# FFN weight preparation in a decoder layer: 16 conversions to bfloat16 moved to GpSimd, 14 PSUM copies moved to ScalarE

## The chip, the cores and the metric

The kernel runs on one core of a Trainium2 chip. The metric is the device time of one execution in microseconds (us). A core has a matrix engine (TensorE, in the profile PE, with its weight loads listed apart as PEld), three engines for elementwise work (VectorE or DVE, ScalarE or ACT, GpSimd or POOL) and a sync engine (SP) that here only issues DMAs. Each engine takes its instructions strictly in the order of the program and waits for the others by semaphores. TensorE writes only to PSUM, which has eight banks; VectorE and ScalarE can read PSUM.

## The reference: what is computed

One decoder layer on x of shape (4, 1024, 256), in float32. Three blocks follow each other, each on a layer norm of x and added to x:

```python
x = x + attn(layernorm(x), w_qkv, w_out)            # 16 heads of 16, windows of 128 plus the window before
x = x + xattn(layernorm(x), ctx, ctx, mask, Wq, ...)  # 77 context rows
x = x + ffn(layernorm(x), clip_x, clip_down, w_gate, w_up, w_down)

def weight_fake_quant(w):                            # in the FFN, per row of w
    scale = max(abs(w), axis=1) / 127
    return clip(round(w / scale), -128, 127) * scale

xq = act_fake_quant(x, clip_x)                       # one scale for the whole tensor
h = act_fake_quant(silu(xq @ wq(w_gate).T) * (xq @ wq(w_up).T), clip_down)
return h @ wq(w_down).T
```

w_gate and w_up are (704, 256), w_down is (256, 704). The quantised weights are whole numbers from -128 to 127, which bfloat16 holds exactly; the row scales are multiplied in later.

## The kernel before

**Two phases.** Up to about 600 us the kernel does self attention (S) and cross attention (X) for four batches; the rest is the FFN. The attention is cut into eight jobs, in the order S0, S1, S2, X0, S3, X1, X2, X3. A job has four groups of four heads, written (g, o), and a group is cut into units: four for S, two for X. There are 96 units, and one slot of the schedule handles one unit, some 4 to 7 us.

**A slot** is written out by hand, in this order of program text, and so of each engine's queue: early layer norms `xn` on GpSimd (L529); then `weighted_values` into a bank `ps_av` for a group whose weights are two slots old, with its copy, normalising and transposes on VectorE (L780 to L802); then `tasks`; then `beside` (work off TensorE); then `put_maxima`, which transposes the row maxima into `ps_mx`, copies them on ScalarE to `mxT` (L683) and writes them by four DMAs on SP into spare rows of `q` (L686); then `max_bias` and `maxima` for the unit five slots ahead: scores into four banks `sc_n`, whose maxima VectorE takes (L657 for S, L668 for X); then `weight_bias` and `weights` for the unit of the slot: scores transposed into four banks `sc_t` (L712 for S; L697 and L741 for X), exp on ScalarE (L722, L744), and for S a causal select on GpSimd (L726). The `bo` additions on GpSimd (L556) come last. The maxima written by `put_maxima` are needed by `weights` in the next slot for an S group, three slots later for X.

**Tasks** have an earliest slot, a due slot and a cost, and the planner fits them in by due time up to a cap of 1.35 a slot on the first list and 1.2 on `beside`. Tasks on TensorE are the projections of q and k (`ps_p`, L583, out of PSUM by two ScalarE operations each, L593 to L599), the values (`ps_v`, L564, by ScalarE, L571), transposes of the normalised input (`ps_t`, L544, one half by VectorE, L548, the other by ScalarE, L550), the output projection (`ps_op`, L811, added to x by VectorE, L820), and the turns described next.

**The FFN weights** are prepared beside the attention by `prep_ffn`, in 14 pieces, one every three slots or so from job S2 on: six row blocks of 128 for w_gate, six for w_up (`rows_of`), two for w_down (`down`). Each piece has four steps. `load` fetches the rows by SP. `scale` (cost 1.0, in `beside`) takes their largest magnitude and its reciprocal on VectorE (L426 to L429). `quant` (cost 1.0, in `beside`) multiplies on VectorE to int8 (L435, into `w8`, which has one buffer) and converts to bfloat16 (L436, into `q_f` or `q_d`, two buffers); for w_down the last 64 columns are copied once more (L482), and the scale is spread to `wide` (L484). `turn` (cost 0.2, a task, due six to seven slots after the load) transposes on TensorE into one bank, `ps_f` for two blocks of 128 (L462) or `ps_d` for six (L489), and copies the bank into `wgT`, `wuT` or `wdT` (L465, L492), which the FFN reads after 600 us. For w_down `wide` is transposed too, into `ps_ds`, and copied by VectorE (L495).

**Banks.** All tiles named `ps_...`, `sc_n` and `sc_t` share the eight banks of one pool. The pool gives a new tile the bank that it reckons to be free first, and the first matmul into it waits for the last reader of the tile before. In the program before, the banks next used after the turns are these: in the slots at 276, 371 and 414 us `ps_f`'s bank goes to the second `sc_t` tile of the same slot and `ps_mx`'s to the fourth; at 291, 315, 429, 447 and 468 us `ps_f`'s or `ps_d`'s goes to the third; at 334 and 346 us to an `sc_n` tile of the next slot.

Of the kernel before, what the change touches and what calls it, by code (L numbers as in the profile page):

```python
# [17 lines left out]
P = 128  # L18
# [6 lines left out]
def decoder_layer(  # L25
# [32 lines left out]
    nc = tc.nc  # L58
    B, S, D = x.shape
    SK = ctx_in.shape[1]  # L60
    FF = w_gate.shape[0]
# [11 lines left out]
    HR = FF - (NF - 1) * P  # L73
# [73 lines left out]
    wdT = fw.tile([P, NF, D], BF16, name="wdT")  # L147
# [51 lines left out]
    with ExitStack() as att:  # L199
# [6 lines left out]
        def bank(name):  # L206
            return ps_b.tile([P, 512], F32, name=name, tag="b")
# [6 lines left out]
        for o in range(NS):  # L214
# [15 lines left out]
            q = wp.tile([P, 1], F32, name=f"qrows{o}")  # L230
# [8 lines left out]
        f = stage.tile([P, P], F32, name="cb_f", tag="stage")  # L239
# [183 lines left out]
        def row_scale(raw, rows, scale_out):  # L423

            a = small.tile([P, 1], F32, name="wamax")
            nc.vector.tensor_reduce(a[:rows], raw, AX.X, ALU.max, apply_absolute_value=True)  # L426
            nc.vector.tensor_scalar(scale_out, a[:rows], 1.0 / QMAX, None, ALU.mult)
            inv = small.tile([P, 1], F32, name="winv")
            nc.vector.reciprocal(inv[:rows], scale_out)  # L429
            return inv  # L430

        def quantise_rows(raw, rows, inv, q):

            q8 = small.tile([P, FF], I8, name="w8", bufs=1)[:rows, : raw.shape[1]]
            nc.vector.tensor_scalar(q8, raw, inv[:rows], None, ALU.mult)  # L435
            nc.vector.tensor_copy(q, q8)  # L436

        def prep_ffn():


            def rows_of(w, dst, sc, f):
                kept = {}

                def load():
                    kept["raw"] = stage.tile([P, D], F32, name="raw_f", tag="stage")
                    if f < NF - 1:
                        nc.sync.dma_start(out=kept["raw"], in_=w[f * P : (f + 1) * P, :])
                    else:
                        for r in (0, HR):
                            nc.sync.dma_start(out=kept["raw"][r : r + HR], in_=w[f * P :, :])  # L450

                def scale():
                    kept["i"] = row_scale(kept["raw"], P, sc[:, f : f + 1])

                def quant():
                    kept["q"] = stage.tile([P, D], BF16, name="q_f", tag="stage_q")
                    quantise_rows(kept["raw"], P, kept["i"], kept["q"])

                def turn():
                    ps = ps_b.tile([P, NC, P], BF16, name="ps_f", tag="b")  # L460
                    for c in range(NC):
                        nc.tensor.transpose(  # L462
                            ps[:, c, :], kept["q"][:, c * P : (c + 1) * P], ident_bf
                        )
                    nc.vector.tensor_copy(dst[:, :, f * P : (f + 1) * P], ps)  # L465

                return [load, scale, quant, turn]

            def down(c):
                kept = {}  # L470

                def load():
                    kept["raw"] = stage.tile([P, FF], F32, name="raw_d", tag="stage")
                    nc.sync.dma_start(out=kept["raw"], in_=w_down[c * P : (c + 1) * P, :])

                def scale():
                    kept["i"] = row_scale(kept["raw"], P, dsc[:, c : c + 1])

                def quant():
                    kept["q"] = stage.tile([P, NF * P], BF16, name="q_d", tag="stage_q")  # L480
                    quantise_rows(kept["raw"], P, kept["i"], kept["q"][:, :FF])
                    nc.vector.tensor_copy(kept["q"][:, FF:], kept["q"][:, FF - HR : FF])  # L482
                    kept["w"] = stage.tile([P, P], F32, name="wide", tag="stage")
                    nc.vector.tensor_copy(kept["w"], dsc[:, c : c + 1].to_broadcast([P, P]))  # L484

                def turn():
                    ps = ps_b.tile([P, NF, P], BF16, name="ps_d", tag="b")
                    for f in range(NF):
                        nc.tensor.transpose(  # L489
                            ps[:, f, :], kept["q"][:, f * P : (f + 1) * P], ident_bf  # L490
                        )
                    nc.vector.tensor_copy(wdT[:, :, c * P : (c + 1) * P], ps)  # L492
                    ps = bank("ps_ds")
                    nc.tensor.transpose(ps[:, :P], kept["w"], ident)
                    nc.vector.tensor_copy(dsc_row[:, c * P : (c + 1) * P], ps[:, :P])  # L495

                return [load, scale, quant, turn]

            pieces = []
            for w, dst, sc in ((w_gate, wgT, gsc), (w_up, wuT, usc)):  # L500
                for f in range(NF):
                    pieces.append(rows_of(w, dst, sc, f))
            return pieces + [down(c) for c in range(NC)]
# [677 lines left out]
        ps = bank("ps_idle")  # L1181
# [289 lines left out]
```

## Time and profile before

| What | us |
|---|---|
| median of three runs (704.75 to 706.25) | 705.66 |
| the profiled execution, its own time | 707.16 |
| its span, first to last instruction | 705.5 |
| TensorE busy | 660.4 |
| VectorE busy | 548.9 |
| ScalarE busy | 364.8 |
| GpSimd busy | 267.3 |

The profile page gives busy time, the span in slices, the chain of waits that ended last, and groups of instructions. A group's line reads: source line, engine, operation, result <- operands, shapes, count, then busy us, mean ns of one, idle us of the engine just before, and what ended most of that idle time. In the chain view a piece is start, length, engine, tile, line. In the timeline a piece is start, length, engine, line, operation, and in brackets the idle time ahead of it with what ended it. A view of waits lists who waited for whom: total us, times, longest. The granted TensorE clock was 0.987 of full speed on average.

### The profile page before, as it was taken

What the parts mean: (1) busy time and instruction counts of PE and PEld (TensorE: products, weight loads), DVE (VectorE), ACT (ScalarE), POOL (GpSimd) and SP (SyncE); (2) the same over time, 40 slices, a digit from 0 to 9 for tenths busy, and PEclk for the clock granted to TensorE, in tenths of its full rate; (3) what the DMA queues carried; (4) which work ended last, traced back from release to release, by engine and by line L of the source; (5) the groups of instructions that cost most, each with busy time, mean ns of one, the idle gap of its engine ahead of it and who ended that gap; (6) DMA issues with size and microseconds to landing.
All of it is one profiled execution on the core that took longest, in us unless ns stands there. A gap on an engine that the chain in (4) does not pass through costs nothing.

```text
span 705.5 us, 17377 instructions
## 1 busy us (share of the span) xinstructions
PE 660.4 (94%) x6470; PEld 402.6 (57%) x6470; DVE 548.9 (78%) x1919; ACT 364.8 (52%) x670; POOL 267.3 (38%) x514
## 2 busy tenths in 40 slices
PE   7989999999999989999999999999999999778787
PEld 4557566667665666654567667544554537334553
DVE  5588778669788798667879977866766868789887
ACT  2544564634556436534464465345445474688391
POOL 4046533627236386700064788234411023111022
PEclk9999999999999999999999999999999999999999
DMA  8000100000000000000000000000000000000047
GB/s 291 8 3 11 35 3 17 3 20 19 12 15 9 10 10 11 20 2 17 3 9 25 26 24 24 3 2 4 17 17 3 18 17 16 0 2 0 1 90 150
DMA packets 18645, 17.02 MB, mean 24 GB/s; under 512 B 3788, under 2 KB 18049, under 8 KB 18561
## 3 DMA queue, kind: packets, MB, share of 16 engines
q1 hardware_dynamic: 16369, 14.08, 6.4%
q0 software_dynamic: 1904, 1.84, 2.1%
q8 instruction: 51, 0.84, 0.5%
q14 instruction: 33, 0.27, 0.1%
q10 hardware_dynamic: 288, 0.00, 0.0%
HBM read 9.35 MB, written 6.03 MB: 22 GB/s over the span
## 4 chain that ended last, share of the span: by engine, by line
PE 73%; DVE 15%; ACT 6%; issue 4%; DMA 1%; POOL 1%; SPq 0%; ACTq 0%; DVEq 0%
PE ps_p L583 12%; PE sc_n L627 8%; PE ps_av L756 8%; PE sc_t L712 8%; PE ps_op L811 7%; PE sc_n L642 4%; PE ps_av L766 4%; PE sc_t L741 3%; PE po L1397 3%; PE ps_v L564 3%; PE sc_t L697 3%; DVE junk L657 2%; PE ps_t L544 2%; DVE bnst L189 2%; PE pg L1288 2%
## 5 line engine op out<-in xcount | busy, mean ns | idle before, releaser
L657 DVE CUSTOM_DVE_ANT_0 junk<-sc_n,cboth 128x256 bf16<-128x256 f32 (+1 forms) x512 | 172.7, 403 | 39.6 <-PE sc_n L627 39.1
L722 ACT ACTIVATE pt<-sc_t 128x512 f32<-128x512 f32 (+1 forms) x256 | 125.3, 577 | 99.4 <-PE sc_t L712 96.8
L726 POOL TENSOR_SCALAR_AFFINE_SELECT pt<-pt 128x256 f32<-128x256 f32 x256 | 102.2, 408 | 117.1 <-ACT pt L722 106.8
L744 ACT ACTIVATE ptx<-sc_t 77x512 f32<-77x512 f32 x128 | 65.4, 591 | 77.4 <-PE sc_t L741 77.4
L712 PE MATMUL sc_t<-q,k 32*128 32x256 f32 (+1 forms) x1024 | 88.1, 381 | 2.3 <-DMA q<-mxT 0.9
L627 PE MATMUL sc_n<-k,q 32*128 32x256 f32 (+1 forms) x1024 | 80.4, 393 | 0.7 <-DVE mx L657 0.7
L668 DVE TENSOR_REDUCE mx<-sc_n 128x4 f32<-128x308 f32 x128 | 52.2, 470 | 37.0 <-PE sc_n L642 36.8
L157 POOL TENSOR_SCALAR ve<-mv 128x4 f32<-128x4 f32 x20 | 4.6, 232 | 197.7 <-DVE mv L191 197.6
L712 PEld LDWEIGHTS sc_t<-q,k 32*128 32x128 f32 x1024 | 67.1, 189 | 13.1 <-ACT q L597 2.3
L529 POOL TENSOR_SCALAR xn<-x,mv,rs 128x256 f32<-128x256 f32 x56 | 70.4, 1262 | 0.0
L627 PEld LDWEIGHTS sc_n<-k,q 32*128 32x128 f32 x1024 | 49.8, 186 | 30.3 <-DVE mx L657 11.0
L583 PE MATMUL ps_p<-xnT,w_s 128*128 128x512 f32 x128 | 62.4, 617 | 2.3 <-DVE mx L657 1.2
L780 DVE STREAM_TRANSPOSE o_sb<-ps_av 128x512 f32<-128x512 f32 x63 | 45.0, 714 | 23.2 <-PE ps_av L756 13.8
L756 PE MATMUL ps_av<-pt,vt 128*32 128x256 f32 (+1 forms) x1152 | 58.8, 347 | 2.4 <-DVE mx L657 2.3
L756 PEld LDWEIGHTS ps_av<-pt,vt 128*32 128x32 f32 x1152 | 34.6, 110 | 30.4 <-DVE mx L657 6.0
L657 DVE DVE_READ_ACCUMULATOR2_ANT mx<- 128x1 f32 x512 | 42.6, 83 | 0.0
L642 PEld LDWEIGHTS sc_n<-kx,q 32*128 32x128 f32 x1024 | 31.5, 186 | 14.5 <-issue 14.5
L697 PE MATMUL sc_t<-mb_t,ident_bf 77*77 77x512 bf16 x128 | 35.3, 379 | 4.0 <-ACT q L593 3.6
L583 PEld LDWEIGHTS ps_p<-xnT,w_s 128*128 128x128 f32 x128 | 22.5, 192 | 28.1 <-issue 17.1
L642 PE MATMUL sc_n<-kx,q 32*128 32x77 f32 x1024 | 36.2, 277 | 0.0
L766 PE MATMUL ps_av<-ptx,vx 77*32 77x512 f32 x256 | 35.2, 604 | 0.6 <-DVE mx L668 0.6
L1304 DVE SCALAR_TENSOR_TENSOR hT<-pu,usc,act 128x512 f32<-128x512 f32 x44 | 30.6, 744 | 6.4 <-ACT act L1303 6.4
(200 smaller groups left out, 1092.2 us busy)
## 6 DMA issues: line engine op xcount, KB each, us to landing
x<-in_x_dram SPq DMA_DIRECT2D x8, 512.0 KB
out_dram<-y SPq DMA_DIRECT2D x9, 256.0 KB
q<-mxT SPq DMA_DIRECT2D x128, 4.0 KB
out_dram<-x SPq DMA_DIRECT2D x7, 256.0 KB
out_dram<-y POOLq DMA_DIRECT2D x7, 256.0 KB, 4.5
w_s<-in_L_attn_w_qkv_dram SPq DMA_DIRECT2D x2, 384.0 KB
raw_d<-in_L_ffn_w_down_dram SPq DMA_DIRECT2D x2, 352.0 KB
raw_f<-in_L_ffn_w_gate_dram SPq DMA_DIRECT2D x5, 128.0 KB
```

The source lines that it names most:

```text
L529: eng.tensor_scalar(xn, xb[job.b][:, t, :], job.st[hf].mv[:, i, 0:1], job.st[hf].rs[:, i : i + 1], ALU.subtract, ALU.mult,)
L583: nc.tensor.matmul(ps, w[:, c, g * P : (g + 1) * P], job.xnT[hf][:, c, :], start=(c == 0), stop=(c == NC - 1),)
L627: nc.tensor.matmul(banks[j][:, (i + 1) * 2 * P - n : (i + 1) * 2 * P], q[r, t * P : (t + 1) * P], k[r, k0 * P : k0 * P + n], start=True, s ...
L642: nc.tensor.matmul(banks[j][:, i * SK : (i + 1) * SK], q[r, t * P : (t + 1) * P], k[r, :], start=False, stop=(i == HT - 1),)
L657: nc.vector.tensor_tensor_reduce(out=junk[:, 2 * P - n :], in0=banks[j][:, (i + 1) * 2 * P - n : (i + 1) * 2 * P], in1=cboth[:, 2 * P - n ...
L697: nc.tensor.matmul(banks[j][:SK], ident_bf[:SK, :SK], mb_t[:, s], start=True, stop=False)
L712: nc.tensor.matmul(banks[j][:, w : w + n], k[r, t * P : (t + 1) * P], q[r, t * P : t * P + n], start=True, stop=True,)
L722: nc.scalar.activation(pt.rearrange("p i a q -> p (i a q)")[:, :w], banks[j][:, :w], AF.Exp)
L726: nc.gpsimd.affine_select(out=pt[:, :, 0, :], in_=pt[:, :, 0, :], compare_op=ALU.is_ge, fill=0.0, base=0, pattern=[[0, 2], [1, P]], channe ...
L744: nc.scalar.activation(pt, banks[j][:SK], AF.Exp)
L756: nc.tensor.matmul(ps[j * SL : (j + 1) * SL, (a0 - t0) * P : (a1 - t0) * P], slot_of(job.vs[kb // 2][:, kb % 2], heads[j]), job.pts[g, o, ...
L766: nc.tensor.matmul(ps[j * SL : (j + 1) * SL, :], slot_of(vx[:, job.b], heads[j]), job.pts[g, o, j, hf], start=True, stop=True,)
```

## The change

Four statements inside the attention change their engine; their operands, order in the text and tiles stay.

```diff
@@ quantise_rows
             nc.vector.tensor_scalar(q8, raw, inv[:rows], None, ALU.mult)
-            nc.vector.tensor_copy(q, q8)
+            nc.gpsimd.tensor_copy(q, q8)
@@ rows_of, turn
-                    nc.vector.tensor_copy(dst[:, :, f * P : (f + 1) * P], ps)
+                    nc.scalar.copy(dst[:, :, f * P : (f + 1) * P], ps)
@@ down, quant
-                    nc.vector.tensor_copy(kept["q"][:, FF:], kept["q"][:, FF - HR : FF])
+                    nc.gpsimd.tensor_copy(kept["q"][:, FF:], kept["q"][:, FF - HR : FF])
@@ down, turn
-                    nc.vector.tensor_copy(wdT[:, :, c * P : (c + 1) * P], ps)
+                    nc.scalar.copy(wdT[:, :, c * P : (c + 1) * P], ps)
```

The first runs 14 times (12 of 256 columns, 2 of 704), the second 12 times (256 columns), the third twice (64 columns), the fourth twice (768 columns). The conversions then wait for VectorE's L435 in GpSimd's queue, the copies for TensorE's transposes in ScalarE's queue. Nothing else differs in the text.

## The prediction

> **What bounds the kernel now.** I read the page first: busy time, then the chain of waits.
>
> ```profile
> PE 660.4 (94%) x6470; PEld 402.6 (57%) x6470; DVE 548.9 (78%) x1919; ACT 364.8 (52%) x670; POOL 267.3 (38%) x514
> ...
> PE 73%; DVE 15%; ACT 6%; issue 4%; DMA 1%; POOL 1%; SPq 0%; ACTq 0%; DVEq 0%
> ```
>
> TensorE is the bound; VectorE holds 15% of the chain that ended last. Next, the groups by line: everything the change touches runs between 222 and 468 us. In the stretch 215 to 475 us the stretch view gives PE 251.84 busy us of 260, DVE 205.77, ACT 129.40, POOL 128.56. PE idles 8 us there, so no relief of another engine can be worth more than that. The chain drawn over the same stretch has 33.0 us of DVE, 2.9 of ACT and none of POOL.
>
> **What the change removes.** The groups that leave VectorE:
>
> ```profile
> L436 DVE CAST q_f<-w 128x256 bf16<-128x256 int8 x12 | 3.8, 320 | 0.4
> ...
> L465 DVE COPY wuT<-ps_f 128x256 bf16<-128x256 bf16 x6 | 1.7, 285 | 2.7 <-PE ps_f L462 2.7
> L465 DVE COPY wgT<-ps_f 128x256 bf16<-128x256 bf16 x6 | 1.7, 281 | 1.3 <-PE ps_f L462 1.1
> ...
> L436 DVE CAST q_d<-w 128x704 bf16<-128x704 int8 x2 | 1.1, 561 | 0.1
> ...
> L492 DVE COPY wdT<-ps_d 128x768 bf16<-128x768 bf16 x2 | 1.1, 544 | 0.0
> ...
> L482 DVE COPY q_d<-q_d 128x64 bf16<-128x64 bf16 x2 | 0.6, 298 | 0.1
> ```
>
> The sum is 3.8 + 1.7 + 1.7 + 1.1 + 1.1 + 0.6 = 10.0 us of VectorE in 30 instructions. But only what stands on the chain can shorten the run. Following the chain over that stretch piece by piece, I find q_f 0.29 + 0.04 + 0.29, q_d 0.60, the 64-wide copy 0.41, wuT 0.20 + 0.20: 2.03 us in five places (near 248, 296, 387, 397 and 435 us). That is the most that can go. The place at 435 us, chain then wait:
>
> ```profile
> 434.36 0.48 DVE w L435
> ...
> 434.86 0.60 DVE q_d L436
> ...
> 435.49 0.41 DVE q_d L482
> 435.90 0.13 DVE wide L484
> 436.03 0.40 DVE mx L668
> ...
> 436.47 1.99 PE ps_op L811 x8
> ```
> ```profile
> PE ps_op L811 <- DVE mx L668: 0.3, 1, 0.3
> ```
>
> 1.01 us of VectorE goes, but TensorE waited only 0.3 us for it: after that PE's own earlier matmuls are late next. So I cap each place by PE's wait there: 248 us: 0.21 (wait of ps_av); 296 us: 0.25 (cast 0.29, PE waited 1.0, so the cast counts); 387 us: 0.24 (ps_av); 397 us: 0.20 (the copy; PE waited 0.4); 435 us: 0.28. Together 1.2 us. One more: at 468 us the fourth bias matmul of sc_t starts 0.30 us late, right after the wdT copy ends at 468.01, since its bank is ps_d's; from ScalarE, by the price below, the copy ends at about 467.8: 0.2 us gained. **Gain 1.4 us**, bounds 0 and 2.2.
>
> **What it adds on POOL.** No row has this cast at this size; the nearest are these.
>
> ```profile
> L1270 ACT COPY xqT<-ps_x 128x1024 bf16<-128x1024 bf16 x6 | 6.0, 996 | 0.0
> ...
> L1251 POOL CAST xq<-v 128x1024 bf16<-128x1024 int8 x7 | 7.3, 1040 | 44.4 <-ACT v L1246 26.0 <-ACT act L1303 10.4 <-issue 6.0
> ...
> L1268 ACT COPY xqT<-ps_x 128x512 bf16<-128x512 bf16 x2 | 1.2, 585 | 1.6 <-DVE xqT L1267 1.6
> ```
>
> The POOL cast runs at 1.02 ns per element and is the same operation, so I take 0.3 us for 256 and 0.75 for 704, plus 0.15 for the 64-wide copy: 12 x 0.3 + 2 x 0.9 = 5.4 us on an engine that is busy half the stretch. Bounds: 0.2 us (a 4-column POOL operation) and 1.27 (xn L529, 256 wide). The cast waits for VectorE's w (L435), and behind it in POOL's queue stand this slot's selects of pt (L726); their results go into ps_av one to two slots later, about 5 us. Going through all 14 casts, POOL is idle or in xn when w ends, and nowhere do the selects slip by more than 0.35 us, but for the slot at 435 us: there xn ends at 436.6, the selects slip to 437.6, end at 439.1, and ps_av reads them at 441.8. The transposes (L462) come 2.5 to 25 us after the cast now; the tightest is the twelfth, w done 424.19, POOL in its power operation until 425.41, cast done about 425.7, transposes at 427.0. At the upper bound it would be 426.7, still in time. So **POOL costs nothing**; cover gone, a late cast holds PE's queue one for one.
>
> A row that speaks against it: one q_f cast took 0.52 us and one 64-wide copy 0.41, both while POOL ran xn, against 0.29 and 0.18 otherwise. The two engines do disturb each other, by 0.23 us. What follows L435 on VectorE in these slots reads PSUM (junk L657, mx L668, x L820), where no row shows such a stretch, so I take nothing, with 0.23 us in each of the five chain places, 1.2 us, as the upper bound.
>
> [...]
>
> **What it adds on ScalarE.** From 512 to 1024 columns the PSUM copy grows from 585 to 996 ns: 0.80 ns a column, 0.38 us at 256 and 0.79 at 768; bounds 0.25 (mxT, 128 wide) and 0.59. In all 12 x 0.38 + 2 x 0.79 = 6.1 us. ScalarE idles half the stretch, but it is in order, and here a queue forms: the copy now stands behind q, k or vt of its slot and ahead of mxT (L683). The next bank users wait. The eleventh copy shows it:
>
> ```profile
> 412.21 0.28 PE L462 MATMUL ps_f<-ident_bf,q_f 128*128 128x128 bf16 x2
> ...
> 412.41 1.45 ACT L593 ACTIVATE q<-ps_p,bq_p,qrows 128x512 f32<-128x512 f32 x2 [2.05 <-PE ps_p L583]
> ...
> 412.52 0.29 DVE L465 COPY wuT<-ps_f 128x256 bf16<-128x256 bf16 x1 [0.47 <-PE ps_f L462]
> ...
> 413.75 0.24 ACT L683 COPY mxT<-ps_mx 32x128 f32<-32x128 f32 x1
> ...
> 414.00 0.95 PE L712 MATMUL sc_t<-q,k 32*128 32x256 f32 x16
> ```
>
> VectorE frees the bank of ps_f at 412.81. ScalarE would reach it at 413.86, after both q, and end at 414.24; mxT ends at 414.5 instead of 413.99. In this slot sc_t of heads 2 and 4 lie in the banks of ps_f and ps_mx, so the fourth, due at about 414.2, starts at 414.5: 0.3 us; and the row writes into q, whose last lands at 418.44 now (the trace's record of landings), come 0.5 later for matmuls that start at 418.27: 0.15 more. The same reading elsewhere: 276 us 0.3 (mxT's bank), 291 us 0.2 (copy ends 291.05 behind q), 315 us 0.35 (behind k and xnT), 371 us 0.2; in the other slots the copy fills a ScalarE gap of 1 to 4 us ahead of the exps, and at 447 us the 0.79 copy meets a bank that wdT on VectorE held as long. **Cost 1.5 us**; bounds 0 (the pool hands out banks in another order once ScalarE frees them, and the wait falls in the next slot) and 2.3 (0.55 at 315, 0.4 at 447, 0.3 at 291 with the banks as they are).
>
> **Sum.** -1.4 + 1.5 = +0.1 us against the profiled execution, 707.16 us (span 705.5). That execution lies 1.5 us above the median of the runs shown, 705.66; I put the difference on the median: **705.8 us**, no change that can be told. About 0.2% (1.4 us) is what a measurement of this kernel can tell from none.
>
> **Rivals.**
> 1. *VectorE's relief comes through.* The banks are handed out differently, no ScalarE wait shows, and the whole chain share goes: -2.0, 703.7 us. For it: VectorE is 79% busy in the stretch and PE's longest waits name it. Against it: PE waited less than VectorE worked at 248, 387 and 435 us.
> 2. *ScalarE's release of the banks becomes the wait* (slower). Place: sc_t L712 and L697 in the slots at 276, 291, 315, 371, 414 and 447 us; price 2.3 us, while VectorE's gain is only the 0.25 to 0.5 of the places where PE waited longest: +1.9, 707.6 us. It decides once the copy ends over 0.3 us after PE wants the bank in more than four slots. For it: at 276, 291 and 414 us sc_t starts within 0.2 us of the end of q or mxT already. Against it: eight of the 14 turns have no q or k in their slot.
> 3. *POOL is late* (slower): a cast over 1.6 us at 425 us, or selects pushed past ps_av; PE loses a slot's slack, 1.5 to 3 us: 707.5 to 708.5. Against it: the 1.04 us row for four times the width.
> 4. *The work was hidden*: neither side counts. That is my forecast with smaller terms, the same time.
>
> **How the numbers follow.** Forecast with rival 4: 0.45; rival 1: 0.20; rival 2: 0.30; rival 3: 0.05. So faster 0.20, same 0.45, slower 0.35: the costs have more places and wider bounds than the gains, whose upper end the chain fixes. Range: low 705.66 - 2.03 = 703.6; high with 2.3 of cost and no gain 708.0, and 0.2 for part of rival 3: 708.2. The forecast's own range is 704.3 to 707.0.
>
> **What would show it.** VectorE 10 us less busy, POOL 5 to 6 more, ScalarE 6 more; L436 on POOL near 0.3 us, L465 on ACT near 0.38. PE's waits for mx at 248, 296, 387, 397 and 435 us shorter by the amounts above; new waits of sc_t for ScalarE near 276, 291, 315, 371 and 414 us; mxT later by about 0.4 at 371 and 414. A POOL cast of over 1 us, a transposing matmul that waits for POOL, or PE waits at places not named here would prove me wrong.

## The result and the profile after

The changed kernel takes 707.19 us (median of 22 executions, 703.83 to 713.90), the kernel before 704.76 us (22 executions, 702.86 to 707.74). The ratio is 1.0039, with a 95% interval of 1.0025 to 1.0054: slower by 0.4%. Two more sittings gave 1.0046 (1.0022 to 1.0071) and 1.0055 (1.0029 to 1.0082). The time lies in the range predicted, 703.6 to 708.2 us, but above the 704.3 to 707.0 of the forecast proper: the forecast was no change, and what came is the slower case.

The page of the changed kernel, busy time and chain of waits:

```profile
PE 661.0 (94%) x6465; PEld 402.8 (57%) x6470; DVE 539.9 (77%) x1889; ACT 370.0 (53%) x684; POOL 273.0 (39%) x530
...
PE 73%; DVE 14%; ACT 6%; issue 4%; DMA 1%; POOL 1%; SPq 0%; ACTq 0%; DVEq 0%
```

The work moved as written: VectorE 9.0 us less, ScalarE 5.2 and GpSimd 5.7 more. Nothing in these two lines tells of a loss. The groups of the moved work (count, busy us, mean ns, idle before):

```profile
L436 POOL CAST q_f<-w 128x256 bf16<-128x256 int8 x12 | 4.8, 396 | 27.3 <-DVE w L435 27.3
L465 ACT COPY wgT<-ps_f 128x256 bf16<-128x256 bf16 x6 | 2.3, 390 | 0.0
L465 ACT COPY wuT<-ps_f 128x256 bf16<-128x256 bf16 x6 | 2.3, 383 | 1.8 <-PE ps_f L462 1.8
L492 ACT COPY wdT<-ps_d 128x768 bf16<-128x768 bf16 x2 | 1.6, 799 | 3.2 <-PE ps_d L489 3.2
L436 POOL CAST q_d<-w 128x704 bf16<-128x704 int8 x2 | 1.5, 767 | 4.5 <-DVE wide L484 4.5
L482 POOL COPY q_d<-q_d 128x64 bf16<-128x64 bf16 x2 | 0.5, 236 | 0.1
```

ScalarE's prices are as estimated (0.38 and 0.79 us); GpSimd's are 0.40 for 0.30, 0.77 for 0.75, 0.24 for 0.15. The timeline of the eleventh copy, whose lines of before the prediction shows:

```profile
409.96 0.28 PE L462 MATMUL ps_f<-ident_bf,q_f 128*128 128x128 bf16 x2
...
410.16 1.45 ACT L593 ACTIVATE q<-ps_p,bq_p,qrows 128x512 f32<-128x512 f32 x2 [1.86 <-PE ps_p L583]
...
411.50 0.37 ACT L465 COPY wuT<-ps_f 128x256 bf16<-128x256 bf16 x1
...
411.75 1.22 PE L712 MATMUL sc_t<-q,k 32*128 32x256 f32 x16
411.75 0.25 ACT L683 COPY mxT<-ps_mx 32x128 f32<-32x128 f32 x1
```

The copy starts only when both q are done, mxT follows it, and the sixteen matmuls of sc_t, 0.95 us before, are spread over 1.22: by the list of banks above, those into the banks of ps_f and ps_mx had to wait. This is the rival of ScalarE's bank release, in one slot.

**Two profiles can't simply be subtracted.** The profiled execution after took 705.09 us, that of before 707.16, though the kernel is slower. The clock record of the traces has stretches of 3.41 us (or 6.8) at half speed, four to seven in an execution, and before's profile has one more. So I compare the start of each matmul with that of the same matmul in another trace. Where nothing differs the offset is flat: between two executions of the kernel before it stays within 0.04 us from 235 to 490 us. Where a wait is new, it steps up.

### The profile page after: what moved, and what is told of

It is laid out like the page before. It is cut to its first block, busy times and chain, and to the rows that moved or that the text cites. A ratio compares the mean times of both kernels' runs of the same rounds, so it can differ in the third digit from the quotient of the medians.

```text
span 703.4 us, 17370 instructions
## 1 busy us (share of the span) xinstructions
PE 661.0 (94%) x6465; PEld 402.8 (57%) x6470; DVE 539.9 (77%) x1889; ACT 370.0 (53%) x684; POOL 273.0 (39%) x530
## 4 chain that ended last, share of the span: by engine, by line
PE 73%; DVE 14%; ACT 6%; issue 4%; DMA 1%; POOL 1%; SPq 0%; ACTq 0%; DVEq 0%
PE ps_p L583 13%; PE sc_n L627 8%; PE sc_t L712 8%; PE ps_av L756 8%; PE ps_op L811 7%; PE sc_n L642 5%; PE ps_av L766 4%; PE sc_t L741 3%; PE po L1397 3%; PE ps_v L564 3%; PE sc_t L697 3%; DVE junk L657 2%; PE ps_t L544 2%; DVE bnst L189 2%; PE sc_n L608 2%
## 5 line engine op out<-in xcount | busy, mean ns | idle before, releaser
L657 DVE CUSTOM_DVE_ANT_0 junk<-sc_n,cboth 128x256 bf16<-128x256 f32 (+1 forms) x512 | 172.7, 402 | 45.1 <-PE sc_n L627 44.5
L744 ACT ACTIVATE ptx<-sc_t 77x512 f32<-77x512 f32 x128 | 65.5, 592 | 74.4 <-PE sc_t L741 74.4
L712 PE MATMUL sc_t<-q,k 32*128 32x256 f32 (+1 forms) x1024 | 89.6, 382 | 1.7 <-DVE mx L657 0.6
L668 DVE TENSOR_REDUCE mx<-sc_n 128x4 f32<-128x308 f32 x128 | 52.2, 470 | 43.8 <-PE sc_n L642 43.8
L529 POOL TENSOR_SCALAR xn<-x,mv,rs 128x256 f32<-128x256 f32 x56 | 70.0, 1256 | 0.0
L657 DVE DVE_READ_ACCUMULATOR2_ANT mx<- 128x1 f32 x512 | 42.4, 83 | 0.0
L766 PE MATMUL ps_av<-ptx,vx 77*32 77x512 f32 x256 | 35.2, 604 | 0.6 <-DVE mx L668 0.6
```

Source lines behind the costliest of these rows:

```text
L529: eng.tensor_scalar(xn, xb[job.b][:, t, :], job.st[hf].mv[:, i, 0:1], job.st[hf].rs[:, i : i + 1], ALU.subtract, ALU.mult,)
L657: nc.vector.tensor_tensor_reduce(out=junk[:, 2 * P - n :], in0=banks[j][:, (i + 1) * 2 * P - n : (i + 1) * 2 * P], in1=cboth[:, 2 * P - n ...
L712: nc.tensor.matmul(banks[j][:, w : w + n], k[r, t * P : (t + 1) * P], q[r, t * P : t * P + n], start=True, stop=True,)
L744: nc.scalar.activation(pt, banks[j][:SK], AF.Exp)
L766: nc.tensor.matmul(ps[j * SL : (j + 1) * SL, :], slot_of(vx[:, job.b], heads[j]), job.pts[g, o, j, hf], start=True, stop=True,)
```

## The experiments

Every kernel ran beside the kernel before, whose medians were 704.81, 704.91 and 704.89 us in the three sittings of the experiments; the first number of the changed kernel is that of the result above. "In the trace" is the sum of the steps of the offset from 240 to 475 us (times of the A/A trace), less what a stretch at half speed cost there. A/A is the kernel before, run against itself.

| kernel | in the trace, us | median, us | ratio (95%) | mean clock |
|---|---|---|---|---|
| A/A | 0 by definition | 704.61 | 0.9999 (0.9982 to 1.0016) | 0.9871 |
| the change | +0.74, +0.67, +0.62 | 707.19, 707.50, 708.84 | 1.0039, 1.0046, 1.0055 | 0.9842, 0.9848, 0.9822 |
| casts only | -0.34 | 704.59 | 0.9994 (0.9975 to 1.0012) | 0.9866 |
| copies only | +1.23, +1.25 | 707.87, 706.63 | 1.0038 (1.0020 to 1.0055), 1.0028 (1.0011 to 1.0045) | 0.9860, 0.9868 |
| seven crowded copies | +1.61 | 706.95 | 1.0027 (1.0002 to 1.0051) | 0.9863 |
| seven free copies | -0.13 | 704.52 | 1.0008 (0.9987 to 1.0030) | 0.9862 |
| casts and free copies | -0.49, -0.54 | 705.20, 703.84 | 0.9997 (0.9983 to 1.0012), 0.9993 (0.9977 to 1.0009) | 0.9860, 0.9872 |
| extra copies in the queue | +1.59 | 706.88 | 1.0031 (1.0011 to 1.0050) | 0.9852 |
| crowded copies doubled | +4.01 | 709.30 | 1.0067 (1.0043 to 1.0092) | 0.9860 |

**The kernel before against itself** (no edit).

> The kernel before, unchanged, timed against itself, so that its granted clock is listed execution by execution. Clock theory (the changed kernel lost 2.4 us because TensorE was granted less clock in its executions; at equal clock the two are alike within 0.5 us): the executions of the kernel before hold a median clock of about 0.987 to 0.988, against the 0.985 of the changed kernel, and the ratio is 1.000 within 0.001. Bank theory (ScalarE's copies hold the banks for which sc_t waits) and POOL theory (a late cast holds the transposes): the same ratio, but the median clock is that of the changed kernel, 0.985.

The same time, and a mean clock of 0.9871 in its 12 executions (0.9871 in 98 of the kernel before). The loss is no matter of where a kernel stands in a sitting.

**The changed kernel again** (no edit).

> The changed kernel again, on the chip of the other three. All theories: 1.003 to 1.005 of the kernel before, 707 us. Clock theory: its median clock is 0.002 or more below that of the kernel before in the same call. Bank and POOL theories: equal clocks, and the 2.4 us still there.

The loss is there, and so is the lower clock: 0.9848. The trace holds 0.67 us of the 2.7. Neither theory alone does.

**Casts only.**

```diff
-            nc.vector.tensor_copy(q, q8)
+            nc.gpsimd.tensor_copy(q, q8)
...
-                    nc.vector.tensor_copy(kept["q"][:, FF:], kept["q"][:, FF - HR : FF])
+                    nc.gpsimd.tensor_copy(kept["q"][:, FF:], kept["q"][:, FF - HR : FF])
```

> Only the casts and the 64-wide copies (L436, L482) go to POOL; VectorE keeps the copies from the bank. My sum: gain at 248, 296, 387 and 435 us, about -1.0 us, nothing on POOL: 0.9985. Bank theory: the same, -1.0 us, since nothing is on ScalarE. POOL theory: +1.5 to +3 us, and the transposes L462 wait for L436. Clock theory: within 0.5 us at equal clock; the time goes with the clock.

No transposing matmul waits for GpSimd: its theory falls. The gains of 0.29 us at 296 and 0.37 at 435 came, but less than the sum of 1.0, because 0.65 us was lost near 371 us and 0.32 of it came back by 408. Part of the loss shows as a wait for a DMA, which the kernel before doesn't have at this place (views of waits, this kernel and the changed one):

```profile
PE sc_t L712 <- DMA q<-mxT: 0.2, 1, 0.2
```
```profile
PE sc_t L712 <- DMA q<-mxT: 0.4, 1, 0.4
```

**Copies only.**

```diff
-                    nc.vector.tensor_copy(dst[:, :, f * P : (f + 1) * P], ps)
+                    nc.scalar.copy(dst[:, :, f * P : (f + 1) * P], ps)
...
-                    nc.vector.tensor_copy(wdT[:, :, c * P : (c + 1) * P], ps)
+                    nc.scalar.copy(wdT[:, :, c * P : (c + 1) * P], ps)
```

> Only the copies from the bank (L465, L492) go to ScalarE; VectorE keeps the casts. My sum: -0.4 (397 and 468 us) + 1.5 = +1.1 us. Bank theory: +2.3 to +3.3 us, all of the loss is here. POOL theory: within 0.5 us of the kernel before. Clock theory: within 0.5 us at equal clock; the time goes with the clock.

All of the loss is here, 3.1 us in this sitting and 1.7 in a later one; the trace has steps of 0.26 to 0.28 us at 276, 291, 315, 334 and 414 us, 0.59 at 371, and 0.11 at 430, and gains of 0.2 each near 296, 387 and 466. But the steps sum to 1.2 us, not 2.3.

**Only the crowded, only the free copies.** A turn is crowded where q, k or vt stands ahead of the copy in ScalarE's queue and the next bank user close behind it.

```diff
-                    nc.vector.tensor_copy(dst[:, :, f * P : (f + 1) * P], ps)
+                    crowded = f in ((2, 3, 4, 5) if dst is wgT else (1, 4, 5))
+                    copy = nc.scalar.copy if crowded else nc.vector.tensor_copy
+                    copy(dst[:, :, f * P : (f + 1) * P], ps)
```

> The kernel before with only seven of the fourteen copies on ScalarE: gate blocks 2 to 5 and up blocks 1, 4 and 5, the turns in which q, k or vt stand ahead of the copy and sc_t behind it. Bank theory (sc_t waits for the bank that ScalarE holds): the waits of the copies-only kernel come back in these slots, 0.25 us each near 272, 286, 310, 330 and 410 us and up to 0.5 near 370, some +1.6 us in the profile, and about all of its loss, 1.003 or more. ScalarE-work theory (fourteen copies cost by their number, through clock or instruction loads): half the loss, +1.5 us, 1.002.

> The other seven copies on ScalarE (gate blocks 0 and 1, up blocks 0, 2 and 3, both of wdT), the crowded ones on VectorE. Bank theory: no wait at 272 to 330 and at 410 us; the gains near 383 to 395 and at 462 us stay, -0.3 to -0.6 us, 0.9993. ScalarE-work theory: +1.5 us, 1.002. Clock: as the kernel before, 0.987, if the waits make the clock fall; 0.986 if ScalarE's work does.

(The second kernel has the two engines exchanged in that line, and wdT's copies on ScalarE.) The place decides, not the number: seven copies make +1.61 us of steps, the other seven -0.13. In measured time the first is slower; the second can't be told from the kernel before, and its small gain shows in the trace alone.

**Casts and free copies together** (the edits of casts only and free copies).

> The seven uncrowded copies on ScalarE and all casts and 64-wide copies on POOL. Bank theory: the gains of both, -0.3 - 0.45 = about -0.8 us, 0.999, the best version of the change so far. ScalarE-work theory: +1.2 us. If the casts make the clock fall together with the copies: +0.5 us.

In the trace it is 0.5 us ahead of the kernel before, somewhat less than expected, because of the same DMA wait near 371 us. Measured, 24 executions in two sittings average 704.50 us against 705.01 of 98 of the kernel before; neither interval leaves out 1. It is the best version found, and no proven gain.

**Extra copies in ScalarE's queue.** VectorE still empties ps_f. The additional copies compute nothing.

```diff
                     nc.vector.tensor_copy(dst[:, :, f * P : (f + 1) * P], ps)
+                    spare = work.tile([P, D], BF16, name="spare", bufs=1)
+                    nc.scalar.copy(spare, kept["q"])
```

> The kernel before, in which ScalarE makes an extra copy of each block of q_f (128 x 256, from SBUF into a spare tile that nobody reads) at the place where the changed kernel has its copy from the bank, while VectorE still empties ps_f: twelve such copies, no bank held longer but ps_mx. Bank theory, ps_f being the bank: nothing at 286, 310 and 330 us (no mxT in these slots), at most 0.25 us each at 272, 370 and 410 us, in all +0.3 to +0.8 us. If mxT's delay is the wait and not ps_f's bank: the full steps at 272, 370 and 410 us. ScalarE-work theory: most of the loss of the copies-only kernel, +2.5 us.

No step at 291, 315 and 334 us, where the slot has no mxT, and full steps of 0.31, 0.33 and 0.30 at 276, 371 and 414. So there are two waits of equal price: for ps_f's bank where the copy itself is late, and for ps_mx's bank (or the rows written from mxT) where mxT is late behind it. Another 0.35 us is lost near 296 us, which no theory named: VectorE's cast L436 takes 0.57 us there, beside GpSimd's `xn`, instead of 0.29, and TensorE's pause grows from 1.01 to 1.36 us; a stretch at half speed follows. The 2.0 us measured are what the theory of ScalarE's work forecast, but the steps of the trace stand at places, and those of the free copies, which are ScalarE work too, sum to -0.13.

**The changed kernel, copies only, and casts with free copies once more** (no new edits).

> The changed kernel once more, for its granted clock. By the traces its waits are worth +0.7 to +0.9 us and the rest of its 2.4 to 2.7 us is clock (0.9844 on average of 34 executions against 0.9872 of 70 of the kernel before). If the clock belongs to the kernel: 0.9845 again, 0.002 or more under the kernel before in the same call, and 1.003 to 1.0045. If it was chance: 0.987, and only the waits are left, 1.001.

> All fourteen copies on ScalarE, casts on VectorE, once more: by its trace +1.5 us of waits, measured +3.1 us, at a mean clock of 0.986. If the clock belongs to it: 1.004 again. If it was chance: 1.002.

> Casts on POOL and the seven uncrowded copies on ScalarE once more. Its trace has 0.65 us less of waits than the kernel before. If the clock goes with the waits: 0.987 and 0.999. If it goes with work moved off VectorE: 0.985 to 0.986 and 1.000 to 1.0005.

The lower clock goes with the changed kernel in all three sittings: 0.9822 this time, 0.9839 over 43 executions against 0.9871. For copies only it stays open: 0.9864 over its two runs. Casts with free copies, 0.9866 over its two, can't be told from the kernel before.

**The crowded copies doubled.** The second copy writes the same values.

```diff
                     copy(dst[:, :, f * P : (f + 1) * P], ps)
+                    if crowded:
+                        copy(dst[:, :, f * P : (f + 1) * P], ps)
```

> The seven crowded copies on ScalarE, each issued twice, the second writing the same values again, so that ps_f's bank and mxT are held up by one copy more, 0.4 us, in each of the seven slots. Bank theory: each of the seven steps grows by 0.35 to 0.4 us, from +1.6 to +4.1 to +4.5 us in the trace, 1.006. If a half-speed stretch of the clock comes with such waits: the mean clock is lower than the 0.9863 of the kernel with the copies issued once, 0.985 or less. ScalarE-work theory: seven copies more cost as much as the first seven, +3.3 us in all.

The five plain steps grow from 0.26 to 0.68 us each, and the sum to +4.01. In the timeline of the eleventh copy the wait now has its name (this kernel's text is longer, so L467 and L469 are the two copies, L687 is the copy to mxT and L716 the matmuls of sc_t):

```profile
413.91 0.37 ACT L467 COPY wuT<-ps_f 128x256 bf16<-128x256 bf16 x1
...
414.31 0.37 ACT L469 COPY wuT<-ps_f 128x256 bf16<-128x256 bf16 x1
...
414.58 0.25 ACT L687 COPY mxT<-ps_mx 32x128 f32<-32x128 f32 x1
414.73 0.87 PEld L716 LDWEIGHTS sc_t<-q,k 32*128 32x128 f32 x12 [0.34 <-ACT wuT L469]
```

The guess about the clock isn't borne out: with 4 us of such waits the clock is 0.9860 (8 executions), no lower than the 0.9863 with the copies issued once and above the 0.985 that the guess asked for.

## Why the prediction went as it did

**Step by step, in the traces.** Steps of the offset in us, at the places that the prediction named (times of the kernel before):

| place | predicted | the change | casts only | copies only |
|---|---|---|---|---|
| 248 | -0.21 | 0 | 0 | 0 |
| 276 | +0.30 | +0.27 | 0 | +0.26 |
| 291 | +0.20 | +0.26 | 0 | +0.26 |
| 296 | -0.25 | -0.55 | -0.29 | -0.23 |
| 315 | +0.35 | +0.28 | 0 | +0.28 |
| 334 | 0 | +0.26 | 0 | +0.26 |
| 371 | +0.20 | +0.96 | +0.65 | +0.59 |
| 387 to 408 | -0.44 | -0.60 | -0.32 | -0.27 |
| 414 | +0.45 | +0.29 | 0 | +0.26 |
| 430 | 0 | +0.11 | 0 | +0.11 |
| 435 | -0.28 | -0.37 | -0.37 | -0.12 |
| 466 | -0.20 | -0.20 | 0 | -0.20 |
| sum, with smaller ones | +0.12 | +0.74 | -0.34 | +1.23 |

**What held.** The gains: predicted 1.38, measured 1.72, in the places named, but for 248 us, where 0.13 came and was lost again. Of the 1.72, 0.23 at 296 us is only delay of 291 us caught up, since copies only, which keeps the cast on VectorE, gets it back too; some 1.5 is gain. So PE's waits were nearly the right cap, and the 2.23 us of the chain (2.03 and the 0.2 at 468 us) were too much. The price of the waits at 276, 291, 315 and 414 us: 1.30 predicted, 1.10 measured. GpSimd's cover held: the view of waits puts two waits of ps_av, 0.4 us each near 246 and 386 us, down to a cast, but TensorE is no later there than in the kernel before. Nor did the casts on GpSimd hinder VectorE: what ran beside them in the changed kernel are L657 and L668, which read PSUM, and their means stayed (420 and 419 ns, 471 and 470), so nothing came of the 0.23 us a place, 1.2 us in all, that the prediction had as its upper bound. Beside other work of GpSimd VectorE was slower in some places, in the kernel before already: L790, from SBUF to SBUF, took 0.42 us with GpSimd idle, 0.42 to 0.55 beside `xn` (L529) alone, and 0.83 at 433 us beside L556 and `xn`. One price was misworked: 1.5 to 3 us for a late POOL is 707.2 to 708.7 us on the median, not 707.5 to 708.5; nothing rests on it.

**What failed: two terms of the step "Cost 1.5 us", whose steps came to 2.4 us in the trace (0.11 of it at 430 us, where none was foreseen), and a term that was missing.**
1. *334 us* was counted among the slots in which the copy "fills a ScalarE gap". But k (L599, twice, 1.45 us) runs there from 0.2 us after the transposes' start, the copy waits for it, and the matmuls of sc_n behind it came 0.26 us later.
2. *371 us*, 0.2 predicted for the bank, 0.96 measured. The rest is the rows that SP writes into q. They land 3.89 us after their first issue in the kernel before, and 4.50 to 4.59 in the changed kernel. What moved is a fetch of instructions: in the DMA record an 8 KB packet of the queue marked "instruction" starts 1.96 us after the first row's issue before and about 3.2 us after it now. Over all fourteen traces the landing goes with that distance: 1.0 to 2.0 us give 3.9, 2.4 to 2.7 give 4.1 to 4.2, 3.1 to 3.4 give 4.5 to 4.8. The casts alone do it too, with mxT no later than before. The link is read from the traces; no experiment moved the fetch by itself.
3. *The clock.* The prediction took TensorE's granted clock as given. Mean times differ by 2.87 us (707.88 over 43 executions, 705.01 over 98), mean clocks by 0.0031. Within the kernels (one slope for all) a clock lower by 0.001 goes with 0.46 us more. By that slope some 1.4 us of the loss is clock, and 1.4 (give or take 0.4) is left at equal clock, of which the steps in the trace explain 0.6 to 0.9. The split depends on the price: a stretch of 3.41 us at half speed is 0.0024 of the mean clock and cost 1.5 us at 484 us, 0.6 us for each 0.001; by that 1.9 us is clock, and the 0.9 left is what the steps show. That the clock is lower is measured; that it makes this part of the loss is argued from these slopes, since no run changed the clock alone.

**Where the clock falls.** The place is at 477 to 485 us, behind the last turn. Timelines of the A/A kernel and of the changed kernel's third profile:

```profile
472.96 2.04 ACT L744 ACTIVATE ptx<-sc_t 77x512 f32<-77x512 f32 x4 [2.51 <-PE sc_t L741]
...
477.97 0.38 PE L697 MATMUL sc_t<-mb_t,ident_bf 77*77 77x512 bf16 x1 [1.00 <-ACT q L593]
...
480.20 1.06 PE L766 MATMUL ps_av<-ptx,vx 77*32 77x512 f32 x8
```
```profile
476.26 2.04 ACT L744 ACTIVATE ptx<-sc_t 77x512 f32<-77x512 f32 x4 [2.79 <-PE sc_t L741]
...
481.27 0.38 PE L697 MATMUL sc_t<-mb_t,ident_bf 77*77 77x512 bf16 x1 [1.28 <-ACT q L593]
...
483.94 1.94 PE L766 MATMUL ps_av<-ptx,vx 77*32 77x512 f32 x8
```

The exps L744 start 0.28 us late. Their semaphore had come in time (475.94 us); in the kernel before the first exp follows its semaphore by 0.04 us, here by 0.32 (0.32 to 0.33 in the other profiles with all fourteen copies), and an 8 KB instruction packet is fetched right after, at 477.2 (in the kernel before such a packet comes only when PE is past this place, 481.5). ScalarE has 14 instructions more by then (831 ahead of this exp, semaphore instructions included, against 817); the kernels with seven copies, with extra and with doubled copies stand at 824, 820 and 802, and none of them has the late start. That the fetch holds the exp is read from this order, not tested. So q comes 0.28 later and TensorE's pause grows from 1.00 to 1.28 us. Then the same eight matmuls L766 take 1.94 us instead of 1.06. The view by stretches for the changed kernel (stretch, its length, busy us and count of PE, PEld, DVE, ACT and POOL, then the granted clock, DMA share, GB/s):

```profile
475.00:480.00 5.00, 4.99 (x31) 1.73 (x24) 3.91 (x11) 3.74 (x9) 2.04 (x2) 1.00 0.03 7
480.00:483.00 3.00, 1.73 (x41) 1.12 (x40) 0.27 (x1) 1.22 (x2) 0.00 (x0) 1.00 0.00 0
483.00:490.00 7.00, 7.00 (x33) 3.27 (x25) 4.24 (x12) 2.77 (x6) 0.94 (x2) 0.51 0.00 1
```

After the pause the clock is 0.51. All five profiles of kernels with all fourteen copies have the pause of 1.28 to 1.30 us here, and three of them a half-speed stretch within 1.8 us of its end, at 1.5 us of time for each 3.4 us; of the nine others, with pauses of 1.00 to 1.01, none has. That is of the size of the missing 1.4 us (6 us in five profiles). But copies only has the same pause, and the stretch in both of its profiles, while its mean clock over 24 executions is 0.9864, hardly under the 0.9871 of the kernel before. So the profiles show where the clock can fall, and not that this place makes the whole of the lower mean clock. What decides in which executions the stretch comes is seen in part only (last section).

**Against the rivals.** ScalarE's bank release was to decide from "more than four slots" with a wait over 0.3 us; there were seven slots, at 0.26 to 0.29 us for most, but the gains were not lost, and about half of the time came with the lower clock. That the result, 707.2 us, lies near this rival's 707.6 is in part luck: its waits alone make +0.74. VectorE's relief was never worth its 2.0 us: casts with the free copies, which pays for few of the waits, gains 0.5 in the trace. The forecast's sum, +0.1, and the trace's +0.74 differ by less than a measurement can tell. That the loss could be measured goes with the clock, which the prediction left out; the range took it in because it was wide.

## What to carry to other kernels

When work goes to an in-order engine, list for each instance what stands ahead of it in that queue and whose bank or buffer it holds: seven of fourteen equal copies cost 1.6 us and the other seven nothing, so move by place and not by kind. Look behind every pause of TensorE that grew for a stretch at half speed: one that grew by 0.28 us had such a stretch behind it in three of five profiles, at 1.5 to 3 us. And take the mean clock over many executions. Compare traces by the offset of equal instructions, since two profiles of one kernel differ by more than the change did.

## What the runs showed of the hardware beyond that

- **Pauses and the clock.** Between 215 and 590 us of all fourteen traces, none of 50 pauses of TensorE from 0.70 to 1.09 us is followed within 4 us by a half-speed stretch; of nine pauses from 1.22 to 1.50 us five are, within 1.8 us. The doubled copies, 4 us of waits in pauses of at most 1.09, had none. Length alone doesn't decide: from 590 to 620 us, of 29 pauses of 1.19 to 1.47 us two are followed within 4 us. In every trace the half-speed stretches begin whole multiples of 3.413 us apart (34.13 and 23.89 us, ten and seven of them, between the first three of the kernel before). Laid on that grid, each of the five followed pauses lies within one cell; of the four others two cross an edge and two (1.22 and 1.28 us) do not. So in these nine pauses it seems to matter where a pause falls on the grid, which differs between executions; it isn't the whole condition.
- **Instruction fetches show.** In the changed kernel's first profile 8 KB packets of the instruction queues went with rows of mxT that landed 4.96 us after their first issue at 250 us and 4.56 at 473, where most take 3.9 to 4.0. In the profile of the kernel before, a 16 KB packet 3.13 us after the first issue at 231 us went with rows that took 5.19 us; in the changed kernel's first profile such a packet came there 3.21 us after the issue, and the rows took 3.92.
- **Prices.** In the changed kernel's first profile GpSimd's casts from int8 to bfloat16 took 0.40 us for 256 columns and 0.77 for 704, ScalarE's bfloat16 copies from PSUM 0.38 to 0.39 us for 256 columns and 0.80 for 768.
